# Two cross-attention blocks: two elementwise steps of Block 1 moved from GpSimd to VectorE, and a third tile for the key counts

## Chip, cores and metric

The kernel runs on one core of a Trainium2 chip. The metric is the device time of one execution in microseconds (us). Before the change it is 2821.14 us, the median of three runs that lie between 2816.69 and 2826.64 us. The engines are named as in the profile: PE is TensorE, DVE is VectorE, ACT is ScalarE, POOL is GpSimd, and SP is the SyncE queue that issues the DMAs.

## The reference

Input x and a context, both 16 x 256 x 512 in fp32, go through two blocks; there are 16 heads of 32. Block 0 attends from the layer-normed x to the layer-normed context under a mask, projects, adds, and runs an MLP of 2048 hidden units with exact gelu. The change lies in Block 1, whose reference is, cut to what matters:

```python
def _mha(x, kv, Wq, Wk, Wv, mask, causal):
    m = mask[:, None]
    Q = einsum('bsd,hdk->bhsk', x, Wq) * m
    K = einsum('bsd,hdk->bhsk', kv, Wk) * m
    V = einsum('bsd,hdk->bhsk', kv, Wv) * m
    energy = einsum('bhsk,bhtk->bhst', Q, K)
    lengths = sum(energy[:, :, 0, :] != 0, axis=-1)
    energy = where(cols >= lengths, -inf, energy)      # and the causal mask, if causal
    score = softmax(energy / sqrt(dk))
    return (einsum('bhst,bhtk->bhsk', score, V) * m)   # heads side by side again

mask0 = 1 - all(x == 0)
x1 = layernorm(x + _mha(x, x, ..., mask0, causal=True), ln1)
mask1 = 1 - all(x1 == 0)
x2 = layernorm(x1 + _mha(x1, context, ..., mask1, causal=False), ln2)
z = (maximum(x2 @ fc1.T + b1, 0) * mask0) @ fc2.T + b2
out = layernorm(x2 + z * mask0, ln3)
```

Three details matter below: each row of the context is multiplied by mask1 before K and V are made from it; the attention's result is added to the rows of x; and the number of keys of a head is a count of the non-zero energies of the first query.

## The kernel before

All matrix products split each fp32 operand into a high and a low part (`split`, L119) and run three matmuls (`mm3`, L255). The 16 batches are taken in eight groups of two, that is 512 rows, four tiles `t` of 128 rows.

Block 0's attention takes the first 700 us or so, its MLP the time to about 1450 us. Block 1's attention lies from about 1450 to 2658 us, and its MLP is the rest. Block 1 has 16 jobs (`Mha`): eight of self-attention, one for each group, to about 1930 us, and then eight of cross-attention. In each job two streams are woven together by `weave` (L330): the attention of one job (`Attention.stream`), and beside it `feed`, which makes the queries, keys and values of the next job. TensorE's program is in the order in which this code is run through (`tc.manual_schedule`). On the other engines, and on the DMA queue of SP, the order is set by the tile scheduler, which runs a timeline of its own; once set, each engine takes its instructions strictly in that order, so that one that waits holds all behind it.

A unit of attention is one batch and one chunk of four heads. For a head, TensorE writes the scores into one of two "sc" banks (L408); DVE takes their minimum (L419 in cross jobs; L423, together with the causal mask, in self jobs); ACT takes the exponential (L433), which frees the bank; three heads later TensorE transposes it (L449) into one of two "pt" banks, ACT (L455), or DVE for a unit's last head in cross jobs (L453), copies it out, and after four heads TensorE mixes the values (L468). Then `scale` (L1300, L1301) prepares the reciprocal sums, `finish` transposes the result (L1313), DVE scales it to `zz` (L1315), and GpSimd adds it to x (L1322). When the four units of a batch are done, `norm` runs the layer norm on its two row tiles: L238, L239, L241 on DVE, the power -0.5 on GpSimd (L242), L251 and L252 on DVE; in self jobs a further DVE instruction finds rows that are all zero (L1218); then the rows are stored (L1291). Later jobs load them again (L1341).

In `feed`, a cross job's context rows are loaded into `cx` (L1401; three buffers of the tag "t512", which are shared with other users), multiplied by the row mask m on GpSimd (L1408), transposed on TensorE (L277) and split by ACT (L132) and DVE (L133). The next `cx` is loaded only after a buffer is free. Queries and keys are split (L127, L128 or L132, L133), stored (L378) and loaded again into the stacks that the scores read (L389, L393). `first_token` (L1227, L1229, L136, L137) and `lengths` make the key counts: TensorE writes the first query's energies into a "pt" bank (L1246), DVE copies one part to the tile `lbias` (L1254) and adds the other (L1255), which frees the bank, counts (L1257), and turns the count into a bias row (L1260 to L1262), which is stored (`dbias`, L1266) and later loaded into a stack (L398). `lbias` comes from the pool "work3", which has two buffers for each tag, so a new count waits until the store of the one before last has been done.

New weights are loaded during the turn from self to cross jobs; their split (L187, L190) runs partly on GpSimd.

Of the kernel before, what the change touches and what calls it, by code (L numbers as in the profile page):

```python
# [10 lines left out]
F32 = mybir.dt.float32  # L11
# [4 lines left out]
ALU = mybir.AluOpType  # L16
# [5 lines left out]
B, S, C, H = 16, 256, 512, 16  # L22
# [3 lines left out]
HPC = P // D  # L26
NB = 2
# [14 lines left out]
def kernel(ctx: ExitStack, tc: tile.TileContext, a, out):  # L42
# [7 lines left out]
    nc = tc.nc  # L50
# [22 lines left out]
    for t, at in ((0, 0), (1, P)):  # L73
        w = (t + 1) * P
        nc.gpsimd.affine_select(
            out=tri[:, at : at + w],
# [10 lines left out]
    for i in range(NB):  # L87
        own = hmask[:, i, i * HPC : (i + 1) * HPC]
        nc.gpsimd.memset(own, 1.0)
        for base, step in ((0, 1), (D - 1, -1)):  # L90
            nc.gpsimd.affine_select(
                out=own,
# [169 lines left out]
    def sbuf(ph, name, bufs, side=None):  # L262
        return ph.enter_context(
            tc.tile_pool(name=name, bufs=bufs, side=side, reuse_waits="tile")
        )
# [4 lines left out]
    def bank(tag, name):  # L270
        return psum.tile([P, 512], F32, tag=tag, name=name, bufs=BANKS[tag])

    def transposed(dst, src, t, tag="mm"):

        ps = bank(tag, "ps_t").rearrange("p (c n) -> p c n", n=P)
        for c in range(KC):
            nc.tensor.transpose(ps[:, c, :], src[:, ts(c, P)], ident)  # L277
        split(ps, (dst[0][:, :, ts(t, P)], dst[1][:, :, ts(t, P)]))
        return 4 * T_PASS
# [243 lines left out]
    class Job:  # L523
        bias = None
# [715 lines left out]
    def lengths(pool, scratch, k, q0, neg):  # L1240


        ps = bank("pt", "ps_e0")[: D + NB * HPC, :S]
        for i in range(NB):
            for x in range(2):
                nc.tensor.matmul(  # L1246
                    ps,
                    q0[:, i, :],
                    k[x][:, ts(i, S)],
                    start=(i == 0 and x == 0),  # L1250
                    stop=(i == NB - 1 and x == 1),
                )
        bias = pool.tile([NB * HPC, S], F32, tag="lbias", name="lbias")
        nc.vector.tensor_copy(bias, ps[D:])  # L1254
        nc.vector.tensor_tensor(bias, bias, ps[: NB * HPC], ALU.add)  # L1255
        n = pool.tile([NB * HPC, 2], F32, tag="n", name="n")
        nc.vector.tensor_scalar(  # L1257
            bias, bias, 0.0, None, ALU.not_equal, ALU.add, accum_out=n[:, 0:1]
        )
        nc.vector.reciprocal(n[:, 1:2], n[:, 0:1])  # L1260
        nc.vector.tensor_scalar(n[:, 1:2], n[:, 1:2], 0.0, neg, ALU.mult, ALU.add)
        nc.vector.tensor_scalar(  # L1262
            bias, cols[: NB * HPC, :], n[:, 0:1], n[:, 1:2], ALU.is_ge, ALU.mult
        )
        d = scratch.tile([NB * HPC, S], F32, tag="dbias", name="dbias")
        nc.sync.dma_start(out=d, in_=bias)  # L1266
        return d


    def block1(mlp0):  # L1270
        tables, more = {}, {}

        class Mha(Job):
# [36 lines left out]
            def finish(self, u):  # L1310
                pz = u.bank[:, S:].rearrange("p (t n) -> p t n", n=P)
                for t in range(NT):
                    nc.tensor.transpose(pz[:, t, :], u.zs[:, ts(t, P)], ident)  # L1313
                zz = pool.tile([P, NT, P], F32, tag="zz", name="zz")
                nc.vector.tensor_tensor(  # L1315
                    zz.rearrange("p t (j d) -> p t j d", d=D),
                    pz.rearrange("p t (j d) -> p t j d", d=D),
                    u.rr.rearrange("p t (j o) -> p t j o", o=1).to_broadcast([P, NT, HPC, D]),
                    ALU.mult,
                )  # L1320
                xv = self.x[:, u.i * NT : (u.i + 1) * NT, ts(u.c, P)]
                nc.gpsimd.tensor_tensor(out=xv, in0=xv, in1=zz, op=ALU.add)  # L1322
                self.left -= 1
                if self.left % KC == 0:
                    for t in range(u.i * NT, (u.i + 1) * NT):
                        att.later.append(lambda t=t: self.norm(t))
                return NT * T_PASS
# [6 lines left out]
        def inputs(tag):  # L1334
            return pair(mlp0.ins, tag)
# [36 lines left out]
        pool = sbuf(ctx, "work3", 2)  # L1372
# [25 lines left out]
        def context_rows(n, t):  # L1398
            if n < len(jobs) and jobs[n].cross and (n, t) not in cxs and t < G:
                cx = cxs[n, t] = pool.tile([P, C], F32, tag="t512", name="cx", bufs=3)  # L1400
                nc.sync.dma_start(out=cx, in_=of("ctx", jobs[n].g)[:, t, :])  # L1401

        def context(n, t):
            job = jobs[n]
            if t == 0:
                job.c_t = inputs("c_t")
            cx = cxs[n, t]
            nc.gpsimd.tensor_scalar(cx, cx, job.m[:, t : t + 1], None, ALU.mult)  # L1408
            cost = transposed(job.c_t, cx, t)
            context_rows(n, t + 3)  # L1410
            return cost
# [20 lines left out]
        def feed(n):  # L1432
# [5 lines left out]
            for c in range(KC):  # L1438
                ps = yield from project_t(w["q"].w, c, job.x_t)
                q, hl = halves(pool, 0, 2)  # L1440
                q0s[c] = first_token(pool, tok0, ps)
                split(ps, hl, scale=-SC if job.cross else None)
                att.keep(job, c, 0, q)
                if job.cross:
                    for t in FRONTS[c]:
                        context_rows(n, t)
                        yield context(n, t)
# [6 lines left out]
            def count(c):  # L1454
                job.bias[c] = lengths(
                    pool, scratch, ks.pop(c), q0s[c], -NEG if job.cross else NEG
                )
                return 4 * 112.0
# [135 lines left out]
```

## Time and profile before

| What | Value |
|---|---|
| Median of three runs | 2821.14 us (2816.69 to 2826.64) |
| The profiled execution's own time | 2812.6 us |
| Span of its trace | 2810.9 us |
| Mean granted TensorE clock | 0.986 of full speed |
| PE busy | 2676.1 us |
| DVE busy | 2045.4 us |
| ACT busy | 1823.0 us |
| POOL busy | 862.1 us |
| L1322 on POOL | 128 instructions, 746 ns each |
| L1408 on POOL | 32 instructions, 1630 ns each |

The span runs from the first to the last instruction of the profiled execution; its own time is the same execution's device time. In a row of the profile's groups, the line of the program, the engine and the operation come first, then what is written and read, with shapes and a count; after the bar the busy time of all of them and the mean duration of one in ns, and after the next bar how long the engine had been idle just before them and which instruction or transfer ended that. In the timeline the two numbers ahead of the engine are the start and the duration in us, and the bracket holds the idle time just before it. In the windows each engine's busy time is followed by its number of instructions; the last three columns are the granted TensorE clock, the share of the DMA engines' time, and GB/s. In the view of waits the three numbers are the total in us, the number of waits and the longest.

### The profile page before, as it was taken

How to read it: one execution, taken by the hardware profiler on the slowest of the kernel's cores; microseconds unless marked ns; L12 is line 12 of the kernel's file. 1: busy time of each engine (PE TensorE's matmuls, PEld its weight loads, DVE VectorE, ACT ScalarE, POOL GpSimd, SP SyncE). 2: the span in 40 equal slices, each digit the busy share in tenths (PEclk: the TensorE clock that was granted, in tenths of full speed). 3: DMA queues.
4: the chain of work that ended last, by engine and by line, in shares of the span. 5: the costliest groups of instructions: out<-in, count | busy, mean ns of one | idle time of the engine just before them, and what ended most of it. 6: DMA issues, size and time to landing. Idle time of an engine off the chain costs nothing.

```text
span 2810.9 us, 56659 instructions
## 1 busy us (share of the span) xinstructions
PE 2676.1 (95%) x18970; PEld 2259.4 (80%) x18970; DVE 2045.4 (73%) x5763; ACT 1823.0 (65%) x5292; POOL 862.1 (31%) x874
## 2 busy tenths in 40 slices
PE   6999999998899999999989999999999999999998
PEld 5777777776799999889887787777777777777787
DVE  7666666657756559888876777777777777777887
ACT  4877777778555555343446787787777777777532
POOL 6222211204601127666661111113322122213333
PEclk9999999999999999999999999999999999999999
DMA  6565555644323334434356665657665555556221
GB/s 230 169 193 175 174 176 171 195 158 143 127 110 135 121 144 171 150 121 150 121 190 213 196 189 182 192 183 222 205 199 172 187 185 186 188 166 183 97 93 58
DMA packets 287810, 465.41 MB, mean 166 GB/s; under 512 B 36257, under 2 KB 188321, under 8 KB 279329
## 3 DMA queue, kind: packets, MB, share of 16 engines
q1 hardware_dynamic: 287520, 461.78, 51.0%
q8 instruction: 153, 2.51, 0.4%
q14 instruction: 137, 1.11, 0.1%
HBM read 284.97 MB, written 176.69 MB: 164 GB/s over the span
## 4 chain that ended last, share of the span: by engine, by line
PE 67%; DVE 15%; DMA 7%; issue 4%; ACT 3%; POOL 3%; SPq 1%; POOLq 0%; DVEq 0%; ACTq 0%
PE ps_p L258 17%; PE ps_v L258 14%; PE ps_pt L449 8%; PE down L1015 5%; PE ps_s L408 5%; PE ps_z L468 5%; PE up_sc L902 3%; DVE c_t L142 3%; PE up_pt L902 2%; PE up_mm L902 2%; PE ps_t L277 2%; DVE st L238 1%; DMA xd<-x 1%; ACT e L433 1%; DVE e L423 1%
## 5 line engine op out<-in xcount | busy, mean ns | idle before, releaser
L433 ACT ACTIVATE e<-e,mn 128x256 f32<-128x256 f32 (+1 forms) x1024 | 487.4, 480 | 66.3 <-DVE mn L423 63.9
L455 ACT COPY pt<-ps_pt 128x512 f32<-128x512 f32 (+1 forms) x696 | 378.2, 546 | 177.5 <-PE ps_pt L449 165.5
L449 PE MATMUL ps_pt<-ident,e 128*128 128x128 f32 x2816 | 437.0, 274 | 21.8 <-DVE lbias L1255 10.0
L449 PEld LDWEIGHTS ps_pt<-ident,e 128*128 128x128 f32 x2816 | 336.3, 141 | 62.9 <-ACT pt L455 7.6
L408 PE MATMUL ps_s<-stack 97*128 97x256 f32 (+1 forms) x1536 | 331.9, 298 | 15.0 <-ACT e L433 7.1
L408 PEld LDWEIGHTS ps_s<-stack 97*128 97x128 f32 (+1 forms) x1536 | 269.5, 190 | 74.5 <-ACT e L433 14.3
L1322 POOL TENSOR_TENSOR x<-x,zz 128x256 f32<-128x256 f32 x128 | 95.5, 746 | 727.9 <-DVE zz L1315 670.2
L1015 PE MATMUL down<-w_h,c_t 128*128 128x256 f32 x900 | 264.5, 295 | 21.5 <-DVE c_t L142 21.5
L433 ACT ACTIVATE e<-ps_s,mn 128x256 f32<-128x256 f32 x512 | 241.0, 483 | 53.9 <-DVE mn L419 43.9
L1015 PE MATMUL down<-w_h,x_t 128*128 128x256 f32 x868 | 254.8, 293 | 11.0 <-ACT x_t L141 8.8
L1015 PE MATMUL down<-w_l,x_t 128*128 128x256 f32 x868 | 253.3, 292 | 0.0
L423 DVE CUSTOM_DVE_ANT_0 e<-mb,ps_s 128x256 f32<-128x256 bf16 x512 | 192.6, 415 | 76.8 <-PE ps_s L408 74.8
L242 POOL TENSOR_TENSOR rstd<-rstd,nhalf 128x1 f32<-128x1 f32 x192 | 140.6, 738 | 316.6 <-DVE rstd L241 314.4
L258 PE MATMUL ps_p<-x_t,q_h 128*128 128x512 f32 x640 | 215.2, 417 | 4.4 <-DVE qk L128 2.3
L419 DVE TENSOR_REDUCE mn<-ps_s 128x2 f32<-128x512 f32 x256 | 175.0, 684 | 48.9 <-PE ps_s L408 46.6
L468 PE MATMUL ps_z<-pt,v 128*32 128x256 f32 (+1 forms) x3072 | 200.1, 369 | 4.3 <-ACT pt L455 2.1
L1015 PEld LDWEIGHTS down<-w_h,c_t 128*128 128x128 f32 x900 | 180.8, 201 | 25.0 <-DVE c_t L142 25.0
L423 DVE CUSTOM_DVE_ANT_0 e<-tri,ps_s 128x128 f32<-128x128 f32 (+1 forms) x512 | 160.1, 346 | 53.5 <-PE ps_s L408 51.4
L433 ACT ACTIVATION_READ_ACCUMULATOR e<-e,mn 128x1 f32 x1024 | 197.4, 193 | 0.0
L1015 PEld LDWEIGHTS down<-w_h,x_t 128*128 128x128 f32 x868 | 175.2, 202 | 12.5 <-ACT x_t L141 10.0
L141 ACT CAST x_t<-sums 128x512 fp32r<-128x512 f32 x156 | 92.6, 619 | 138.0 <-DVE sums L791 89.6
L1015 PEld LDWEIGHTS down<-w_l,x_t 128*128 128x128 f32 x868 | 175.0, 202 | 0.0
(245 smaller groups left out, 7463.6 us busy)
## 6 DMA issues: line engine op xcount, KB each, us to landing
stack<-d SPq DMA_DIRECT2D x1152, 128.0 KB
d<-qk SPq DMA_DIRECT2D x192, 512.0 KB
hid<-ho SPq DMA_DIRECT2D x32, 1024.0 KB
raw<-hid SPq DMA_DIRECT2D x32, 1024.0 KB
x<-xd SPq DMA_DIRECT2D x128, 256.0 KB
xd<-x SPq DMA_DIRECT2D x96, 256.0 KB
xin<-in_x_dram SPq DMA_DIRECT2D x32, 256.0 KB
xin<-in_ctx_dram SPq DMA_DIRECT2D x32, 256.0 KB
```

The source lines that it names most:

```text
L242: nc.gpsimd.tensor_tensor(out=rstd[:, 1:2], in0=rstd[:, 0:1], in1=nhalf, op=ALU.pow)
L258: nc.tensor.matmul(ps, w[p], x[q], start=(k == 0 and i == 0), stop=(k == kc - 1 and i == 2))
L408: nc.tensor.matmul(ps[:, t, :], u.st[: self.rows, 0, j, ts(t, P)], u.st[: self.rows, 1, j, :], start=True, stop=True,)
L419: nc.vector.tensor_reduce(mn, ps, AX.X, ALU.min)
L423: nc.vector.tensor_tensor_reduce(out=e[:, at], in0=bias[t], in1=ps[:, t, : job.width[t]], scale=-SC, scalar=BIG, op0=ALU.add, op1=ALU.min, ...
L433: nc.scalar.activation(e[:, at], ps[:, t, :] if bias is None else e[:, at], AF.Exp, bias=mn[:, t : t + 1], scale=-1.0, accum_out=u.rs[:, t ...
L449: nc.tensor.transpose(pp[:, ts(x, P)], e[:, at : at + P], ident)
L455: nc.scalar.copy(pt[:, :n], pp[:, :n])
L468: nc.tensor.matmul(z[ts(j, D), w[0] * P :], job.v[u.i * NT + mc][:, u.c * P + j * D : u.c * P + (j + 1) * D], u.pt[j][:, x0 * P : (x0 + le ...
L902: nc.tensor.matmul(ps[:, mm, :], w[p][:, k, :], x[q][:, k, :], start=(first and mm == k == j == 0), stop=(k == 1 and j == 2), skip_group_c ...
L1015: nc.tensor.matmul(ps[:, t, :], x[p][:, mm, ts(t, P)], w[r][:, bo, :], start=(q == mm == t == j == 0), stop=(q == self.NS - 1 and mm == 1 ...
L1322: nc.gpsimd.tensor_tensor(out=xv, in0=xv, in1=zz, op=ALU.add)
```

## The change

There are three edits, all in Block 1. `lbias` gets three buffers instead of two. The addition of `zz` to the rows (128 instructions of 128x256) goes from GpSimd to VectorE. The multiplication of the context rows by their mask (32 instructions of 128x512) goes from GpSimd to VectorE. The operations and their data are the same. TensorE's order stays as it was; VectorE has 160 instructions more, GpSimd 160 fewer, and the scheduler, which now sees other times, places some instructions of VectorE, ScalarE and the DMA queue elsewhere.

```diff
@@ lengths
-        bias = pool.tile([NB * HPC, S], F32, tag="lbias", name="lbias")
+        bias = pool.tile([NB * HPC, S], F32, tag="lbias", name="lbias", bufs=3)
         nc.vector.tensor_copy(bias, ps[D:])
         nc.vector.tensor_tensor(bias, bias, ps[: NB * HPC], ALU.add)
@@ Mha.finish
                 xv = self.x[:, u.i * NT : (u.i + 1) * NT, ts(u.c, P)]
-                nc.gpsimd.tensor_tensor(out=xv, in0=xv, in1=zz, op=ALU.add)
+                nc.vector.tensor_tensor(xv, xv, zz, ALU.add)
                 self.left -= 1
@@ context
             cx = cxs[n, t]
-            nc.gpsimd.tensor_scalar(cx, cx, job.m[:, t : t + 1], None, ALU.mult)
+            nc.vector.tensor_scalar(cx, cx, job.m[:, t : t + 1], None, ALU.mult)
             cost = transposed(job.c_t, cx, t)
             context_rows(n, t + 3)
```

In the new order of VectorE, as the built program has it, the four masks of a cross job stand after L128, after L1301, after L1322 and after L1315; the fourth stands directly ahead of the L1322, L419 and L453 that follow. In SP's new order the four loads of x (L1341) of such a stretch stand ahead of the loads of a stack, where before they stood after them and around the load of a `cx`.

## Prediction

> **What bounds the kernel now.** I read the busy times first, then the chain that ended last, then the windows of Block 1's three stretches (self-attention, the turn from self to cross, cross-attention), then POOL's groups, the waits, and the instructions of one burst. The page:
>
> ```profile
> PE 2676.1 (95%) x18970; PEld 2259.4 (80%) x18970; DVE 2045.4 (73%) x5763; ACT 1823.0 (65%) x5292; POOL 862.1 (31%) x874
> PE 67%; DVE 15%; DMA 7%; issue 4%; ACT 3%; POOL 3%; SPq 1%; POOLq 0%; DVEq 0%; ACTq 0%
> ```
>
> TensorE is busy for 95% and is most of the last chain; POOL, from which work is taken, is 3% of it, while DVE, to which it goes, is 15%. The windows, columns PE, PEld, DVE, ACT, POOL, then clock:
>
> ```profile
> 1450.00:1930.00 480.00, 469.84 (x3331) 380.26 (x3332) 350.69 (x1594) 364.24 (x1236) 77.48 (x96) 1.00 0.64 200
> 1930.00:2010.00 80.00, 70.88 (x509) 56.86 (x508) 56.23 (x242) 57.54 (x198) 37.16 (x40) 0.96 0.70 213
> 2010.00:2658.00 648.00, 631.51 (x4514) 500.17 (x4514) 505.30 (x1273) 474.06 (x1525) 156.87 (x162) 1.00 0.56 175
> ```
>
> TensorE is idle for 10.2, 9.1 and 16.5 us there: 36 us bound any gain, since its own order is the same before and after. DVE is at 73 to 78% on average. POOL's two groups, from the view of Block 1's POOL instructions, and three waits of the same window:
>
> ```profile
> L1322 POOL TENSOR_TENSOR x<-x,zz 128x256 f32<-128x256 f32 x128 | 95.5, 746 | 727.9 <-DVE zz L1315 670.2 <-DVE n L1261 38.9 <-DVE own L1229 7.7
> L1408 POOL TENSOR_SCALAR cx<-cx,m 128x512 f32<-128x512 f32 x32 | 52.1, 1630 | 65.7 <-DMA cx<-in_ctx_dram 53.1 <-PE ps_s L408 7.8 <-PE ps_pt L449 1.9
> ```
>
> ```profile
> POOL cx L1408 <- DMA cx<-in_ctx_dram: 53.1, 20, 6.5
> PE ps_pt L449 <- DVE lbias L1255: 10.0, 9, 3.9
> DVE lbias L1254 <- DMA dbias<-lbias: 8.1, 7, 2.2
> ```
>
> POOL waits 53.1 us for context rows, at no cost as long as nothing urgent stands behind. On DVE something does.
>
> **What the Trainium skill says.** "VectorE: DVE Perf Modes", section on the TRN2 errata, gives fp32 tensor_tensor as (N+151)/0.96 ns: 424 ns for N=256. The row of L137 with two SBUF inputs of 128x256 has 476 ns, L1315 (one PSUM input) 420, so the trace roughly agrees. Its tier table gives tensor_scalar in fp32 on SBUF twice the rate; the trace's cast L136 of 128x512 takes 423 ns, while L247, with two per-row operands, takes 610. "SBUF — State Buffer", section "Who interferes with whom", says that DVE and GpSimd share a port pair that one of them holds for a whole instruction. L251 has 805 ns on average against 730 to 740 where POOL is idle, which fits, though its cause isn't shown. So POOL's lighter load may return a little.
>
> **Part 1, the third lbias tile.** In the turn, views of TensorE and of DVE:
>
> ```profile
> 1959.39 0.52 PE L449 MATMUL ps_pt<-ident,e 128*128 128x128 f32 x3 [3.85 <-DVE lbias L1255]
> ```
>
> ```profile
> 1957.84 0.42 DVE L1254 COPY lbias<-ps_e 8x256 f32<-8x256 f32 x1 [2.18 <-DMA dbias<-lbias]
> ```
>
> The copy L1254 waits for the store of an older tile; the add L1255 frees the count's "pt" bank, for which TensorE's transposes wait 3.85 us. With three tiles this DMA wait goes: 2.18 us at most. But in DVE's new order two rows' cx stand ahead of that copy, and POOL's starts put their landings at 1953.9 and before 1956.2, so about 1.2 of it is kept. In self-attention the same wait appears twice with about 0.96 us of TensorE; the new order puts other work between L1254 and L1255, so half: -1 us for both.
>
> **Part 2, x += zz (L1322) on DVE.** 128 instructions leave POOL (95.5 us at 746 ns) and cost DVE 128 x 0.42 = 54 us of busy time, beside TensorE except in bursts. Lower bound 0.34 each (the start-to-start time of L1315), upper 0.48 (L137's row). In a self job, DVE is late around the norms (TensorE stalls of 0.59 and 0.27 us near 1811): the add puts 0.34 there, while the order moves one L252 of 0.66 behind a score reduction. First stall +0.07, second -0.36: -0.3 a job, x7 = -2 us (bounds -5 to +2). The norms no longer wait for POOL (4.3 us of L238's idle), but most of that is under other work.
>
> **Part 3, the context mask (L1408) on DVE.** 32 instructions, 52.1 us on POOL, become 32 x 0.42 = 13.5 us; bounds 0.36 and 0.61 each. Parts 2 and 3 add 67 us: DVE goes from 912 to 979 of 1208 us, 76 to 81%. On average that is covered; in the burst of each cross job it isn't. POOL and DVE of one:
>
> ```profile
> 2211.36 1.57 POOL L1408 TENSOR_SCALAR cx<-cx,m 128x512 f32<-128x512 f32 x1 [5.29 <-DMA cx<-in_ctx_dram]
> 2212.90 1.08 POOL L242 TENSOR_TENSOR rstd<-rstd,nhalf 128x1 f32<-128x1 f32 x2
> 2227.07 1.56 POOL L1408 TENSOR_SCALAR cx<-cx,m 128x512 f32<-128x512 f32 x1 [1.46 <-DMA cx<-in_ctx_dram]
> ```
>
> ```profile
> 2213.50 1.41 DVE L252 SCALAR_TENSOR_TENSOR x<-x,rstd,ln 128x512 f32<-128x512 f32 x2 [0.33 <-POOL rstd L242]
> 2217.11 0.68 DVE L453 COPY pt<-ps_pt 128x512 f32<-128x512 f32 x1
> 2225.31 0.69 DVE L419 TENSOR_REDUCE mn<-ps_s 128x2 f32<-128x512 f32 x1 [0.51 <-PE ps_s L408]
> 2225.92 0.68 DVE L453 COPY pt<-ps_pt 128x512 f32<-128x512 f32 x1
> ```
>
> From 2207 to 2219 DVE has no gap above 0.33 us. Three cx (3 x 0.36) and one L1322 (0.33) come in ahead of the copy L453 at 2217.11, on which the mix L468 at 2218.26 waits: 1.4 us later. Against it: the power L242 no longer stands behind a 1.57 us mask on POOL, which gives back the 0.33 gap, and slack to the mix is 0.5 to 0.7. So +0.4 us a burst.
>
> The fourth cx is the **added wait**. It landed when POOL took it, 2227.07; in DVE's new order it stands after L1315 (2224.37), ahead of L1322, the reduction L419 at 2225.31 and the copy L453 at 2225.92. If DVE waits, L419 starts at 2227.07 + 0.36 + 0.34 = 2227.8, 2.5 late. Its exponentials still free the score bank before the next score at 2230.22, but L453 would end at 2229.1, and the mix at 2227.72 waits for it: +1.4. If the transfer lands a little sooner, nothing is lost. It may: SP's new order issues the four x loads (L1341) before a stack's loads instead of around this cx, so less moves beside it; but the first x load then waits for the stores L1291, and cx may be issued later. I take +0.35. The stack loads behind those x loads are not needed by TensorE for another two units (some 12 us of cover). A burst: +0.75, six of them +4.5 us; without overlap or luck 2.3 each. In the first cross jobs three waits of 1 to 3 us fall in slack or against the later L1218: 0.
>
> **The turn.** 1930 to 2010 has POOL at 46%, with the new weights' casts between masks. Third tile -1.2; one cx of 1.57 us no longer behind a cast -1.2; powers and counts less delayed -1.6: -4 (bounds 0 to -9, its idle time).
>
> **Sum**: self -1 - 2 = -3; turn -4; cross +4.5; together -2.5 us. Against the profiled execution's 2812.6 that is 2810.1; the runs' median is 2821.14, 8.5 above it within their spread, and the difference carries over: **2818.6 us**. The final MLP, Block 0 and its MLP hold none of the edited lines.
>
> **The rivals.**
> A, small net change (as summed): own range 2811 to 2827, from -10 to +6.
> B, faster: cx lands before DVE reaches it and DVE's slack takes the rest, so cross gives 0 to -4, the turn -8, self -6: -17 on average, 2804 (2796 to 2812). For it: 9.1 us idle in the turn with POOL at 46%, and POOL's 1.57 us per mask. Against: DVE without gaps in the bursts.
> C, slower: DVE is held by cx at the head of its queue. Place: third and fourth cx of each burst. Price: 0.7 to 1.1 plus 1.4, some 2.3 a burst, x6 = 14, and 3 to 4 in the first cross job; less 3 of gains: +15, 2836 (2830 to 2842). It decides where cx lands more than about 1.1 us (L453's slack to its mix) after DVE has reached it; before, the fourth landed 2.3 us after L1315's end. Against it: in other bursts the next reduction isn't yet due.
> D, the edits land where TensorE never waits and nothing shows: within A.
>
> **How the numbers follow.** A 0.45, B 0.32, C 0.23. A measurement of this kernel can tell about 0.3% from no change, 8.5 us: faster is below 2812.7, slower above 2829.6. Of A, 0.04 lies below and 0.03 above; B and C are nearly whole: faster 0.35, same 0.40, slower 0.25. The range leaves out about a tenth on each side: 2799 (inside B, a little above its best end) to 2838 (C's middle and a little). A cx of 0.61 instead of 0.42 would add under 2 us and is inside.
>
> **What would show it.** Right: no wait of L1254 for dbias; TensorE's idle in the turn down to about 5 us; DVE near 979 us; a wait of DVE for cx of up to 2 us at the fourth cx of a burst. Wrong: such waits of under 0.5 us (then B), or TensorE's transposes or mixes waiting for L453 by 1 us or more in every burst (then C); lbias waits that stay although a tile is free, so the bank and not the tile was the limit.

## The result, and the profile after

The changed kernel takes 2836.28 us in the median of four runs (2832.07 to 2836.47), the kernel before 2819.0 us in the median of four: a ratio of 1.006 with a 95% interval of 1.0042 to 1.0077, about 17 us more. That is slower by more than the 0.3% that the prediction set as its bound, near the 2836 that it gave for its rival C, and not the small change that it held likeliest. The profiled execution of the changed kernel has a span of 2834.5 us, 23.6 more than the one before; the latter's own time, 2812.6 us, lies below all four runs of its kernel, so differences between the two profiles come out some us too large.

From the changed kernel's page, the busy times and the chain that ended last, by engine and by line:

```profile
PE 2689.6 (95%) x18970; PEld 2263.9 (80%) x18970; DVE 2091.4 (74%) x5923; ACT 1821.2 (64%) x5292; POOL 721.1 (25%) x714
...
PE 66%; DVE 15%; DMA 8%; ACT 4%; issue 4%; POOL 2%; SPq 1%; POOLq 0%; DVEq 0%; ACTq 0%
PE ps_p L258 17%; PE ps_v L258 14%; PE ps_pt L449 8%; PE ps_z L468 5%; PE down L1015 5%; PE ps_s L408 5%; DVE c_t L142 3%; PE up_sc L902 3%; PE up_pt L902 2%; DMA cx<-in_ctx_dram 2%; PE ps_t L277 2%; PE up_mm L902 2%; DMA d<-qk 2%; ACT e L433 1%; DVE st L238 1%
```

DVE has 46 us more and POOL 141 less, while TensorE is busy for 95% as before, so the sum of work alone does not explain the loss. The chain by line, in the last row, says more: the load of the context rows (`cx<-in_ctx_dram`) has 2% of it, 52 us, against 14 us in the chain of before. The three windows of Block 1:

```profile
1450.00:1930.00 480.00, 471.44 (x3339) 380.76 (x3338) 366.01 (x1656) 364.86 (x1252) 41.59 (x48) 1.00 0.65 200
1930.00:2010.00 80.00, 73.98 (x527) 58.28 (x526) 64.02 (x267) 59.03 (x204) 23.18 (x23) 0.96 0.73 214
2010.00:2658.00 648.00, 611.88 (x4316) 480.57 (x4315) 508.68 (x1307) 459.75 (x1477) 56.06 (x58) 0.99 0.56 170
```

TensorE's idle time fell from 10.2 to 8.6 us in self-attention and from 9.1 to 6.0 in the turn, and rose from 16.5 to 36.1 in the last stretch. Windows of fixed times drift against the program, so the rest of this document uses stages cut at the same TensorE instructions: its order is the same in all these kernels, and the starts of the score matmuls (L408) numbered 512, 896, 1088 (counted from 0) and the last divide Block 1. A job has 64 of them, so the first stage is the first six self jobs, the second the last two self jobs with the first cross job, and the third the other seven cross jobs. (The scores of self-attention run on to 2034 us; the 1930 us given above lie inside the seventh self job.) Each cell has the length in us and, after the stroke, TensorE's idle time in it; the kernels below the first two are the experiments.

| Kernel | Six self jobs | Two self jobs, first cross job | Seven cross jobs |
|---|---|---|---|
| before | 399.1 / 7.1 | 223.7 / 13.8 | 520.0 / 11.7 |
| changed | 395.3 / 3.9 | 226.4 / 14.2 | 545.4 / 27.9 |
| e1 tile only | 396.6 / 5.3 | 225.4 / 15.0 | 523.7 / 13.7 |
| e2 addition only | 395.1 / 3.8 | 229.0 / 16.9 | 529.7 / 12.4 |
| e3 masks only | 399.1 / 7.3 | 224.0 / 14.3 | 536.2 / 24.0 |
| e4 tile and addition | 395.3 / 3.9 | 224.9 / 14.0 | 527.9 / 12.2 |
| e5 changed, row tile 2 on POOL | 395.3 / 4.0 | 225.4 / 14.3 | 531.0 / 17.7 |
| e6 before, row tile 2 on DVE | 398.0 / 6.3 | 225.4 / 13.6 | 530.1 / 17.8 |
| e7 changed, masks held back | 395.4 / 4.0 | 222.1 / 12.8 | 530.6 / 17.6 |
| e8 e7, row tile 3 on POOL | 395.4 / 4.0 | 223.3 / 12.3 | 524.7 / 10.4 |
| e9 tile, addition in self jobs | 395.3 / 3.9 | 224.7 / 14.2 | 526.2 / 15.0 |
| e10 e9, masks held, tile 3 on POOL | 395.4 / 4.0 | 220.9 / 10.6 | 521.8 / 13.5 |
| e11 changed, row tile 3 on POOL | 395.4 / 3.9 | 225.6 / 14.0 | 527.9 / 11.6 |

The self jobs gained 3.8 us, as forecast within 1 us. Nearly all of the loss is in the seven cross jobs: 25 us. Where in a job is seen in one burst, the stretch of a cross job in which the masks, the last steps of a norm and the copies for the mixes come close together. DVE in the changed kernel (start, duration, engine, line; in the bracket the idle time before it and what ended that):

```profile
2227.92 0.42 DVE L1315 TENSOR_TENSOR zz<-ps_z,rr 128x256 f32<-128x256 f32 x1 [0.15 <-PE ps_z L1313]
2232.01 0.49 DVE L1408 TENSOR_SCALAR cx<-cx,m 128x512 f32<-128x512 f32 x1 [3.67 <-DMA cx<-in_ctx_dram]
2232.41 0.42 DVE L1322 TENSOR_TENSOR x<-x,zz 128x256 f32<-128x256 f32 x1
2232.75 0.68 DVE L419 TENSOR_REDUCE mn<-ps_s 128x2 f32<-128x512 f32 x1
2233.35 0.68 DVE L453 COPY pt<-ps_pt 128x512 f32<-128x512 f32 x1
```

and TensorE beside it:

```profile
2231.26 0.63 PE L468 MATMUL ps_z<-pt,v 128*32 128x256 f32 x6
2234.08 1.05 PE L468 MATMUL ps_z<-pt,v 128*32 128x256 f32 x10 [2.19 <-DVE tok L1227]
```

DVE stands still for 3.67 us at the head of its queue. Behind it the copy L453 ends at 2234.0, and the mix, begun at 2231.26, breaks off after six matmuls and goes on at 2234.08, as soon as that copy is out. (The bracket names L1227, the instruction after the copy. A releaser is inferred, and the copy is the one that the mix reads.) The next scores start 2.8 us later against before than the scores ahead of the mix. All this for rows that nobody needed: this is row tile 2 of the *next* job, whose transposes come about 60 us later.

In the five full bursts, this one wait is 4.03, 3.67, 2.47, 3.33 and 2.94 us, together 16.4 us of the 28.3 that DVE waits for context rows in all of Block 1 (total, times, longest). With the starts of TensorE's instructions set side by side in the two kernels, the five mixes behind it are 12.4 us longer.

```profile
DVE cx L1408 <- DMA cx<-in_ctx_dram: 28.3, 19, 4.0
```

A second loss is at the first scores of a burst. In the kernel before TensorE waits there for 0.30 us, in the changed one for 1.60 (TensorE of before, then of the changed kernel):

```profile
2215.07 0.50 PE L408 MATMUL ps_s<-stack 97*128 97x256 f32 x2 [0.30 <-ACT e L433]
```

```profile
2218.70 0.51 PE L408 MATMUL ps_s<-stack 97*128 97x256 f32 x2 [1.60 <-ACT e L433]
```

No transfer is involved here. On DVE of the changed kernel, ahead of the reduction that these scores wait for by way of the exponential:

```profile
2214.73 0.70 DVE L252 SCALAR_TENSOR_TENSOR x<-x,rstd,ln 128x512 f32<-128x512 f32 x1
2215.35 0.68 DVE L133 TENSOR_TENSOR c_t<-ps_t,c_t 128x512 fp32r<-128x512 f32 x1
2215.95 0.74 DVE L252 SCALAR_TENSOR_TENSOR x<-x,rstd,ln 128x512 f32<-128x512 f32 x1
2216.61 0.17 DVE L137 TENSOR_TENSOR tok<-own,tok 128x16 fp32r<-128x16 f32 x1
2216.69 0.68 DVE L419 TENSOR_REDUCE mn<-ps_s 128x2 f32<-128x512 f32 x1
```

Two last steps of the norm (L252) stand ahead of the reduction. In the order before they stood behind it; there their power (L242) was queued on POOL behind a mask of 1.57 us. Over the seven cross jobs this costs the first scores 9.5 us. These two losses are 21.9 of the 25.4 us; smaller gains and losses make up the rest, and one of these, from the addition, is shown at e2.

The DMA queue's order, too, has a new wait. In the waits of the SP queue from 2110 to 2658 us, the changed kernel has

```profile
SPq L1341 <- DMA xd<-x: 11.0, 5, 2.7
```

The loads of x, moved ahead, wait for the stores of the norm's rows. In the burst above the load of row tile 2 is issued at 2227.22, 2.3 us after the transposes that free its buffer (2224.32 + 0.60), against 0.9 us before (2222.28 after 2220.76 + 0.60); from there to the mask's start it is 4.8 us in both.

### The profile page after: what moved, and what is told of

It is laid out like the page before. It is cut to its first block, busy times and chain, and to the rows that moved or that the text cites. A ratio compares the mean times of both kernels' runs of the same rounds, so it can differ in the third digit from the quotient of the medians.

```text
span 2834.5 us, 56545 instructions
## 1 busy us (share of the span) xinstructions
PE 2689.6 (95%) x18970; PEld 2263.9 (80%) x18970; DVE 2091.4 (74%) x5923; ACT 1821.2 (64%) x5292; POOL 721.1 (25%) x714
## 4 chain that ended last, share of the span: by engine, by line
PE 66%; DVE 15%; DMA 8%; ACT 4%; issue 4%; POOL 2%; SPq 1%; POOLq 0%; DVEq 0%; ACTq 0%
PE ps_p L258 17%; PE ps_v L258 14%; PE ps_pt L449 8%; PE ps_z L468 5%; PE down L1015 5%; PE ps_s L408 5%; DVE c_t L142 3%; PE up_sc L902 3%; PE up_pt L902 2%; DMA cx<-in_ctx_dram 2%; PE ps_t L277 2%; PE up_mm L902 2%; DMA d<-qk 2%; ACT e L433 1%; DVE st L238 1%
## 5 line engine op out<-in xcount | busy, mean ns | idle before, releaser
L449 PE MATMUL ps_pt<-ident,e 128*128 128x128 f32 x2816 | 437.6, 274 | 16.5 <-ACT pt L455 6.7
L242 POOL TENSOR_TENSOR rstd<-rstd,nhalf 128x1 f32<-128x1 f32 x192 | 144.7, 760 | 1206.4 <-DVE rstd L241 1204.9
L449 PEld LDWEIGHTS ps_pt<-ident,e 128*128 128x128 f32 x2816 | 336.7, 141 | 57.9 <-ACT pt L455 10.4
L408 PE MATMUL ps_s<-stack 97*128 97x256 f32 (+1 forms) x1536 | 332.7, 298 | 25.6 <-ACT e L433 12.5
L408 PEld LDWEIGHTS ps_s<-stack 97*128 97x128 f32 (+1 forms) x1536 | 269.5, 190 | 86.7 <-ACT e L433 25.0
L468 PE MATMUL ps_z<-pt,v 128*32 128x256 f32 (+1 forms) x3072 | 210.2, 372 | 11.9 <-DVE pt L453 6.8
L419 DVE TENSOR_REDUCE mn<-ps_s 128x2 f32<-128x512 f32 x256 | 174.5, 682 | 34.3 <-PE ps_s L408 32.1
L468 PEld LDWEIGHTS ps_z<-pt,v 128*32 128x32 f32 x3072 | 86.6, 110 | 114.9 <-issue 23.9
```

Source lines behind the costliest of these rows:

```text
L242: nc.gpsimd.tensor_tensor(out=rstd[:, 1:2], in0=rstd[:, 0:1], in1=nhalf, op=ALU.pow)
L408: nc.tensor.matmul(ps[:, t, :], u.st[: self.rows, 0, j, ts(t, P)], u.st[: self.rows, 1, j, :], start=True, stop=True,)
L419: nc.vector.tensor_reduce(mn, ps, AX.X, ALU.min)
L449: nc.tensor.transpose(pp[:, ts(x, P)], e[:, at : at + P], ident)
L468: nc.tensor.matmul(z[ts(j, D), w[0] * P :], job.v[u.i * NT + mc][:, u.c * P + j * D : u.c * P + (j + 1) * D], u.pt[j][:, x0 * P : (x0 + le ...
```

## The experiments

Three theories went into the first series. W: DVE is held at the head of its queue by context rows in transit. O: the added work itself does not fit. S: the DMA queue's order is at fault. A fourth, P, came of it: POOL's release of the power moves the norm's last steps ahead of the reductions. Each time is a median; the ratio is to the kernel before on the same chip, with its 95% interval.

**e1: the third tile alone.**

```diff
-        bias = pool.tile([NB * HPC, S], F32, tag="lbias", name="lbias")
+        bias = pool.tile([NB * HPC, S], F32, tag="lbias", name="lbias", bufs=3)
```

> Only the third lbias tile, the two steps stay on GpSimd. Three theories of the slowdown are tried in this series. W: VectorE is held at the head of its queue by the transfer of a context row (mainly row tile 2 of the next job) in each cross job. O: VectorE's 67 us of added work no longer fit into the bursts, whoever waits. S: the new order of the DMA queue, with the x loads behind the stores and ahead of a stack, delays what TensorE needs. Here all three say the same, a gain of the wait for the store: 3 to 6 us below before, some 2815. It sizes part 1; if it shows nothing, the gain of the turn in the changed kernel came from the masks leaving GpSimd.

Measured: 2813.62 against 2817.05 us, ratio 0.9983 (0.9975 to 0.9992). As expected: part 1 is worth 3.4 us. In the profile it is in self-attention (2.5 us shorter, 1.8 us less idle), and not in the turn.

**e2: the addition alone.**

```diff
-                nc.gpsimd.tensor_tensor(out=xv, in0=xv, in1=zz, op=ALU.add)
+                nc.vector.tensor_tensor(xv, xv, zz, ALU.add)
```

> Only the addition on VectorE, no third tile, the mask stays on GpSimd. W: 0 to 6 us below before. O: 54 of the 67 us, 8 to 14 us above before. S: as W. With the run that has the third tile as well it tells what the tile adds.

Measured: 2822.4 against 2816.69 us, 1.0019 (1.0008 to 1.003). None of the three had it right: no gain, and half of what O asks. Its self jobs are 4 us shorter and the loss is later. TensorE's idle time in the other cross jobs is only 0.7 us above before while the stage is 9.7 us longer, so most of it is not idle time; in this execution the granted clock is 0.91 in the turn and 0.96 in one window of 80 us.

Another part is lost in TensorE's time without showing as idle, because the records of a mix overlap: when the matmuls of one head start late within it, TensorE still counts as busy. Here is the same mix with the copy L453 that it reads, in the kernel before and then in e2:

```profile
2281.50 0.67 DVE L453 COPY pt<-ps_pt 128x512 f32<-128x512 f32 x1
2282.44 1.07 PE L468 MATMUL ps_z<-pt,v 128*32 128x256 f32 x16
```

```profile
2281.98 0.67 DVE L453 COPY pt<-ps_pt 128x512 f32<-128x512 f32 x1
2282.33 1.43 PE L468 MATMUL ps_z<-pt,v 128*32 128x256 f32 x16
```

In e2 the addition and a step of the norm that stood behind the copy before (L238) are ahead of it on DVE; the copy ends 0.32 us after the mix has begun, not 0.27 before, and the mix takes 0.36 us longer. Two mixes of most cross jobs are longer by about as much, some 5 us in all, in each kernel that has the addition on DVE in cross jobs, and in none of the others. So a loss of the kind that O means is there. Its net size is smaller, as other steps come earlier; e8 and e10 below give a size. The rest of the 5.7 us is taken up below.

**e3: the masks alone.**

```diff
-            nc.gpsimd.tensor_scalar(cx, cx, job.m[:, t : t + 1], None, ALU.mult)
+            nc.vector.tensor_scalar(cx, cx, job.m[:, t : t + 1], None, ALU.mult)
```

> Only the context mask on VectorE, no third tile, the addition stays on GpSimd. The DMA queue has the order of the changed kernel. W: 15 to 23 us above before (2834 to 2842), as the held VectorE is here without the gains of the other parts. O: the mask is 13.5 of the 67 us of added work, so 3 to 5 us above before. S: as W, 15 us or more above.

Measured: 2831.57 against 2817.05 us, 1.0043 (1.0028 to 1.0058): 14.5 us more, just under the ranges of W and S, and far above O. Both losses of the changed kernel are in its profile: the mixes behind row tile 2 are 8.7 us longer than before, the first scores 7.8 us later. The three parts alone add up to -3.4 + 5.7 + 14.5 = 16.8 us, about the 17 of the whole.

**e4: the tile and the addition, masks left on POOL.** The edits of e1 and e2 together.

> The changed kernel with the context mask left on GpSimd: third tile and the addition on VectorE. The DMA queue has the order of before. W: 4 to 12 us below before, some 2811. O: 54 of the 67 us of added work are still there, so 8 to 14 us above before, some 2831. S: as W.

Measured: 2816.28 against 2817.05 us, 0.9996 (0.9988 to 1.0005). O falls as the cause of the 17 us: 54 of the 67 us of added work are there and the time is that of before. W's gain didn't come either, which agrees with e1 and e2 within their spread: the tile's gain is taken up by the addition's loss. Without the masks on DVE there is no slowdown.

**e5: the changed kernel, the mask of row tile 2 back on POOL.**

```diff
-            nc.vector.tensor_scalar(cx, cx, job.m[:, t : t + 1], None, ALU.mult)
+            (nc.gpsimd if t == 2 else nc.vector).tensor_scalar(cx, cx, job.m[:, t : t + 1], None, ALU.mult)
```

> The changed kernel with the mask of row tile 2 alone (8 of the 32) back on GpSimd; the DMA queue keeps the order of the changed kernel. W: 12 to 18 us below the changed kernel, some 2820, and no TensorE stall of over 1 us at the mix after it. O: 3.4 of the 67 us are gone, so 2835. S: 2836, since the order of the DMA queue is that of the changed kernel.

Measured: 2823.74 against 2817.05 us, 1.0019 (1.0007 to 1.0031). Some 12 us of the 17 are gone with 8 instructions of 0.5 us each, though the DMA queue kept the changed kernel's order (but for 12 of 2130 places). So neither O nor S by itself is the cause of these 12 us. DVE's wait for context rows in the cross jobs falls from 19.6 to 0.7 us; TensorE's 1.60 us at the first scores stay.

**e6: the kernel before, the mask of row tile 2 alone on DVE.** The edit of e5 with the engines exchanged.

> The kernel before with the mask of row tile 2 alone (8 of the 32) on VectorE; the DMA queue keeps the order of before, so that one wait is all that is added. W: the wait of some 2.3 to 3 us at the head of VectorE's queue in each of six bursts, less a slack of about 1 us: 8 to 15 us above before, some 2830. O: 3.4 us of added work: no change within 2 us. S: no change.

Measured: 2824.26 against 2816.69 us, 1.0025 (1.0014 to 1.0035): 7.6 us, where O and S expect none; W is right in kind and its expected size (8 to 15) a little high. DVE in the cross jobs:

```profile
DVE cx L1408 <- DMA cx<-in_ctx_dram: 10.3, 5, 3.1
```

Five waits, 2.1 us on average, and 6.1 us more of idle TensorE. With the changed kernel's DMA order the same wait was 3.3 us on average. So the DMA order seems to lengthen the wait by about 1.2 us, but no run changed that order alone.

**e7: the changed kernel, with the masks held back until their rows have long landed.**

```diff
             if t == 0:
                 job.c_t = inputs("c_t")
+                z = pool.tile([P, 1], F32, tag="mz", name="mz")
+                nc.vector.tensor_scalar(
+                    z, job.x_t[1].bitcast(F32)[:, 0, N - 1 : N], 0.0, None, ALU.mult
+                )
+                mt = job.mt = pool.tile([P, G], F32, tag="mt", name="mt")
+                nc.vector.tensor_scalar(mt, job.m, z, None, ALU.add)
             cx = cxs[n, t]
-            nc.vector.tensor_scalar(cx, cx, job.m[:, t : t + 1], None, ALU.mult)
+            nc.vector.tensor_scalar(cx, cx, job.mt[:, t : t + 1], None, ALU.mult)
```

> The changed kernel with all masks on VectorE, but with the column of masks of a job made dependent, by adding a zero, on the last split of the job's own rows (16 tiny VectorE instructions more), so that the masks of row tiles 0 to 2 stand in VectorE's queue some 50 us after their rows have landed. The work of VectorE and the order of the DMA queue are those of the changed kernel. W: 12 to 20 us below the changed kernel, 2816 to 2824. O: 2836 or a little above. S: 2836.

Measured: 2816.98 against 2816.69 us, 1.0 (0.9989 to 1.0011). All 32 masks are on DVE, which even has 16 instructions more, the loads of x keep the changed kernel's place ahead of a stack, and the 17 us are gone: W. Some 4 of them are gone from the second stage, where the waits for rows of the first cross jobs go too. DVE's masks of row tiles 0 to 2 (here line 1414) now come in a row, without a wait:

```profile
2261.80 0.85 DVE L1414 TENSOR_SCALAR cx<-cx,mt 128x512 f32<-128x512 f32 x2
2262.64 0.48 DVE L1414 TENSOR_SCALAR cx<-cx,mt 128x512 f32<-128x512 f32 x1
```

What remains in each cross job is 1.60 us at the first scores, as in the changed kernel.

**e8: e7 with the mask of row tile 3 on POOL.** The edit against e7:

```diff
-            nc.vector.tensor_scalar(cx, cx, job.mt[:, t : t + 1], None, ALU.mult)
+            (nc.gpsimd if t == G - 1 else nc.vector).tensor_scalar(
+                cx, cx, job.mt[:, t : t + 1], None, ALU.mult
+            )
```

> The kernel with all masks held back (third tile, addition on VectorE, masks of row tiles 0 to 2 on VectorE some 50 us after their landing), but with the mask of row tile 3 back on GpSimd. What the first series left: with the masks held, each cross job still has a TensorE stall of 1.3 us more than before, at its first scores. Theory P: with GpSimd free of that mask the power of the norm comes earlier, and VectorE's order puts the two last steps of the norm (L252, 0.7 us each) ahead of a score reduction. With the mask of row tile 3 on GpSimd those steps stand behind that reduction again. P: the stall goes, cross-attention loses some 6 us of idle time, 2811. Theory O: the stall comes of VectorE's added work in the burst; of that only 8 x 0.4 us are gone, so 2816.

Measured: 2810.19 against 2815.39 us, 0.9982 (0.9973 to 0.9992). As P expected. TensorE at the first scores, and DVE ahead of them (its lines between the two left out):

```profile
2212.10 0.51 PE L408 MATMUL ps_s<-stack 97*128 97x256 f32 x2 [0.29 <-ACT e L433]
```

```profile
2209.46 0.68 DVE L419 TENSOR_REDUCE mn<-ps_s 128x2 f32<-128x512 f32 x1
...
2210.75 1.41 DVE L252 SCALAR_TENSOR_TENSOR x<-x,rstd,ln 128x512 f32<-128x512 f32 x2 [0.53 <-POOL rstd L242]
```

The reduction stands ahead of both L252 again. That these wait 0.53 us for POOL costs nothing here; that they came early cost 1.3 us a burst, 7.8 us over the cross jobs of e7's profile. The loads of x also went back behind a stack's loads with this edit, so the gain in time is not P's alone for certain; but what the first scores wait for involves no transfer, and their wait is back at its old length.

**e9: tile, masks on POOL, addition on DVE in self jobs only.** The edit of e1, and:

```diff
-                nc.gpsimd.tensor_tensor(out=xv, in0=xv, in1=zz, op=ALU.add)
+                (nc.gpsimd if self.cross else nc.vector).tensor_tensor(out=xv, in0=xv, in1=zz, op=ALU.add)
```

> Third tile, all masks on GpSimd as before, the addition on VectorE in the self-attention jobs alone (64 of 128). The self jobs should have the idle time of the changed kernel (3 us less than before), and the cross jobs that of before. W and P: 3 to 7 us below before, 2811 to 2814, and a little below the kernel that has the addition on VectorE everywhere. O: 27 of the 67 us of added work in place, 2 to 5 us above before less the tile's 3.4.

Measured: 2812.36 against 2815.39 us, 0.999 (0.9975 to 1.0006). The median is where W and P put it, but the interval takes in no change.

**e10: e9 with the held masks of e8.**

> As the kernel with the addition on VectorE in self jobs alone, but with the masks of row tiles 0 to 2 on VectorE, held back till some 50 us after they have landed, and that of row tile 3 on GpSimd. GpSimd has 24 masks of 1.6 us less, of which those of the turn stood between the casts of the new weights. W and P: the turn gains 2 to 4 us, cross is as before, 2808 to 2812. O: no better than with all masks on GpSimd.

Measured: 2807.8 against 2815.39 us, 0.9971 (0.996 to 0.9982): 7.6 us below before and the fastest of all. It differs from e8 only in that the cross jobs' addition is on POOL: the medians, on one chip, differ by 2.4 us, the last stage in the profiles by 2.9. So the addition on DVE costs some 3 us in cross jobs, though the intervals of the two ratios overlap. Row tiles 0 to 2 are masked on DVE where there is time, tile 3 stays where it keeps the norm's order, and the addition moves only where it helps.

**e11: the changed kernel, the mask of row tile 3 back on POOL, nothing held.** The edit of e5 with `t == G - 1`.

> The changed kernel with the mask of row tile 3 alone (8 of 32) back on GpSimd; the masks of row tiles 0 to 2 stay on VectorE and are not held back. The built order has the last steps of the norm behind a score reduction again, and the DMA queue in the order of before. Theory P with W: the stall at a cross job's first scores falls from 1.6 to some 0.3 us, and VectorE's wait for row tile 2 goes on, at some 2 us instead of 3.3, as in the kernel with that mask alone on VectorE; together 7 x 1.3 + 6 x 1 = 15 us below the changed kernel, 2821. If the order of the DMA queue has no part in the length of that wait: 9 below, 2827. Theory W alone, without P: at most 6 below, 2830 or more.

Measured: 2818.45 against 2817.02 us, 1.0013 (1.0 to 1.0025). More than expected came back. The order of DVE shows why the expectation was too careful: the mask of row tile 2 now stands *behind* the copy L453, where the wait for its rows (5.2 us in all in the cross jobs) holds nothing that TensorE needs. TensorE's wait at the first scores is 0.30 us again (at 2212.21), as P has it. But since mask, norm and DMA order all moved, this run does not tell their shares apart.

## Why the prediction failed, step by step

- **Bound, TensorE's idle time of 36 us, and the sum of work on DVE.** Right as far as they go. L1322 takes 431 ns on DVE (0.42 taken), L1408 501 (0.42 taken, within the bounds). DVE's busy time rose by 46 us, less than the 67 of the sum. e4 and e7 show that the work as such is covered but for some us: e8 and e10 put the addition's part in cross jobs at about 3.
- **Part 1.** The waits for the store are gone, and e1 gives 3.4 us. The prediction's sum for it, 2.2 us, was a little low, and its place was wrong: in e1's profile the self jobs have all of the gain and the turn has none.
- **Self jobs.** -3 forecast, -3.8 measured.
- **The turn.** -4 forecast; the stage around it became 2.8 us longer (226.43 against 223.65). The 3.85 us at L1255 are gone and TensorE is up to 13 us ahead of before near 1977 us. Then it stands for context rows:

```profile
1981.01 1.11 PE L277 MATMUL ps_t<-ident,cx 128*128 128x128 f32 x4 [3.30 <-DVE cx L1408]
```

  and DVE waits 1.89 and 0.98 us for two more in the next job, which the prediction put at 0. A gain that runs ahead to a transfer is given back there.
- **The fourth cx.** This is the step that failed most. The place, the wait and the instructions behind it were named rightly, but +0.35 us a burst was taken, in the hope that the rows land sooner. They did not: the same 4.8 us from the load's issue to the mask, and an issue 1.4 us later behind the moved x loads. The loss was 2.8 us in the burst shown and 12.4 over the five. Nor did the prediction ask when these rows are needed: they are for the next job, so the mask could have stood behind the copy at no cost, as it does in e11.
- **The power.** Booked as giving back 0.33 us a burst. It cost 1.3: "earlier on POOL" became "ahead of the score reduction on DVE". The prediction used the new order for the position of the masks; that the same order has L252 ahead of L419 in cross jobs is not in it.
- **The rivals.** C (2836, 0.23) had the place and the price: 2.3 us a burst for waits, against 16.4 us of wait in five bursts and some 12 us of time shown by e5. That its total, 2836, was met so closely is partly luck: the norm's order, which it did not have, gave a part of it. B fell because both its premises, rows in time and slack in DVE, did.

What stays open: the rest of the 5.7 us that the addition alone (e2) costs, beyond the longer mixes. In the profiles of e2 and e4 a wait of DVE of 2.3 us for the power, with a mask ahead of it on POOL, is followed by a stretch in which the granted clock is lower (0.76 in the 10 us from 2370 in e2). Whether such a stop brings the lower clock was not tried. For these reasons the stage lengths above exceed their idle times by some us, and single stages should not be read to better than that. Open, too, is what the DMA queue's order alone is worth.

## What to carry to other kernels

A busy engine that takes its instructions in order should not be given one that waits for a transfer, unless nothing behind it is urgent: the idle engine's 53 us of waiting were free, and 28 us of the same on the busy one cost most of 17 us of run time. Before moving such a step, look up when its result is needed; if that is much later, hold the step back by a dependency and keep the move. And when an engine is relieved, read in the new order what now comes earlier, for it may stand ahead of what the bottleneck waits for.

## What was not expected of the hardware

The mask of 128x512 with one value for each row takes 501 ns on DVE (469 at the least) where a cast of the same shape takes 423, so a price from the cast is too low. On GpSimd it is 1568 ns in the median: moving it makes it 3.1 times as fast, moving the addition of 128x256 (746 to 431 ns) 1.7 times. Relieving GpSimd of 141 us gave DVE's own instructions nothing that shows: in Block 1, L251 went from 743 to 738 ns and L252 from 733 to 741. The prediction took L251's mean of 805 ns as a sign of sharing, but the median is 742; most of the difference comes from five records of over 1.8 us in the final MLP, and the changed kernel has five of these too. So the shared port pair of which "SBUF — State Buffer", section "Who interferes with whom", speaks was no cost that these means show.
